# Accumulator banks for a, joined output blocks, low parts one block later: a reordering of a two-layer float32 kernel

## The chip, the cores and the metric

The kernel runs on one core of a Trainium2 chip. A core has five engines that run side by side: TensorE (PE in the profile) multiplies matrices and writes to PSUM, a memory of eight banks; VectorE (DVE), ScalarE (ACT) and GpSimd (POOL) work on elements; SyncE (SP) issues most DMAs. [...] The metric is the device time of one execution in microseconds (us).

## What is computed

Four sequences of 512 tokens of width 512 go through a slot attention of 16 heads and then through a gated feed-forward layer, each behind a layernorm and with the input added:

```python
def attn(x, Wq, Wk, Wv, Wg, Ws, Wo, gw):       # x normalised, per sequence
    q, k, v = x @ Wq, x @ Wk, x @ Wv           # heads of 64, 64, 128
    s = clip(x @ Ws, -32, 32)                  # 64 slots a head
    z = cumlogsumexp(s, over=tokens)
    g = exp(shift(z) - z); p = exp(s - z)
    hk[t] = hk[t-1] * g[t] + k[t] p[t]^T       # 64 x 64 state
    ok[t] = (q[t] * 64**-0.5) @ hk[t]
    pv = softmax(ok)
    hv[t] = hv[t-1] * g[t] + p[t] v[t]^T       # 64 x 128 state
    o[t] = pv[t] @ hv[t]
    o = o * rsqrt(mean(o*o) + 1e-5) * gw
    o = o * silu(x @ Wg)
    return o @ Wo

def ffn(x):                                    # weights rounded to fp8
    h = silu(x @ q8(gate) * gs) * (x @ q8(up) * us)
    return h @ q8(down) * ds

x = x + attn(layernorm(x), ...)
x = x + ffn(layernorm(x), ...)
```

## The kernel before, in words

**Units.** Attention is done in units (g, b): a pair of heads g (0 to 7) for a sequence b. The order is (0,0), (0,1), (1,0), (1,1), ... (7,1), and then the same for sequences 2 and 3: 32 units. first_unit() (L854) builds (0,0), attention() (L919) the other 31. The values of two pairs of heads are projected together, so units with even g also make values (L644), four blocks of 128 tokens, and last longer. The feed-forward layer follows for all four sequences.

**Precision.** A float32 matrix is split into a high and a low part (fp32r) and a third mixture of both. A projection is eight 128x512 matmuls (high and low, main()) into one bank and four (mixed()) into another; ScalarE copies the first with a factor and VectorE subtracts the second. So each projection takes two of the three "proj" banks, in turn. The weights are split on the chip the first time: load_matrix() (L233) puts a "_" item (the high part of the first piece, on ScalarE) and then pieces (two VectorE instructions and the next high part) into a queue in the program, `work`. The parts of a normalised block are made in layernorm()'s parts() (L357): low = source minus high, mixture, and then ScalarE scales the low part in place.

**Inside a unit.** slots, keys, queries project s, k and q. turn_e and turn_k transpose them (e, kn). key_states (L672) makes three running sums of k p^T, sk. query_key (L677) makes the products within a block, a, two banks of four 128x128 blocks, which VectorE masks with a triangle. slot_scores takes sk, a and e to ok; softmax (okn) and softmax_exp give weights, slot_weights turns them back (w, wT). weight_slot (L736) is to the weights what query_key is to the keys: b, two banks, masked by VectorE. read_out (L739) sums the output ov of the unit: twelve small matmuls with the states (L748), sixteen with b (L757). The output of a unit is finished inside the next: scale_output and scale_other scale ov's banks into og, turn_output (oT) transposes them and multiplies with the gate, high_output, split_output and low_output make the three parts, and project_output(n) (L825) multiplies block n with w_o: four ps_o and two ps_o_m. add_output(n) (L846) subtracts and sends the block to DRAM by an adding DMA.

**Order.** The whole program is scheduled by hand: each engine executes its instructions in the order in which Python calls issue them, and waits where a semaphore asks. Between the stages, other() (L167) takes items from `work` (pace[0] of them, 1 or 2), piece() (L172) takes items until one whose name doesn't end with "_", and need(key) (L180) all that are left of a kind. steps holds the transposes of a norm for the next sequences; next_step() does one. turned() says that the first item belongs to a normalised block (its name begins with xs_).

**Banks.** bank() (L110) gives the next of three PSUM banks in turn: for all transposes, key and value states, a and b. A transposed block of a norm keeps its bank until its parts are made; `held` makes parts() run before that bank is given out again. ps2 is a pool of two accumulator banks, "acc", in turn: ok takes one, ov two; in the feed-forward layer the sums of its output.

Of the kernel before, what the change touches and what calls it, by code (L numbers as in the profile page):

```python
# [49 lines left out]
def kernel(  # L50
# [116 lines left out]
    def other(count=None):  # L167
        for _ in range(count or pace[0]):
            if work:
                work.pop(0)[1]()  # L170
# [131 lines left out]
    def load_tokens(b, source, pool=one, tag="tokens"):  # L302

        x1[b] = pool.tile([P, NT, D], F32, tag=tag, name=f"x1_{b}")
        nc.sync.dma_start(x1[b], source[b].rearrange("(n p) d -> p n d", p=P))

    xs = {}
    whole = []

    def layernorm(b, which, n_bank=None, between=None):  # L310
# [46 lines left out]
        def parts(n):  # L357
            cols = slice(n * P, (n + 1) * P)
            hi, lo = dst[0][:, :, cols].bitcast(F32), dst[1][:, :, cols]
            src = pts[n]  # L360
            if start:
                src = whole[0][:, :, cols]
                nc.scalar.mul(dst[0][:, :, cols], src, UNDER)
            nc.vector.tensor_tensor(lo, src, hi, ALU.subtract)
            if which == 1:
                nc.vector.scalar_tensor_tensor(
                    dst[2][:, :, cols], lo.bitcast(F32), -1.0 / DELTA, hi, ALU.mult, ALU.add
                )
                nc.scalar.mul(lo, lo.bitcast(F32), 1.0 / DELTA)

        if start:
            for n in range(NT):
                measure(n)
                if n > 0:
                    normalise(n - 1)
                    transposes(n - 1)
                if n == 2:
                    between()
            normalise(NT - 1)
            transposes(NT - 1)  # L380
            return [(f"xs_{b}", lambda n=n: parts(n)) for n in range(NT)]
        key = f"xn{which}_{b}_"
# [197 lines left out]
    def diagonal_blocks(lT, rT, name):  # L580

        pa = [bank(f"ps_{name}_{h}").rearrange("p (n t) -> p n t", n=NT) for h in range(HG)]
        for n in range(NT):
# [270 lines left out]
    def first_unit():  # L854
# [15 lines left out]
        transposing = layernorm(1, 1)  # L870
        work.extend(parts)
        load_matrix("g", 0, True)
        X.values(1)
        other(3)
# [21 lines left out]
        next_step()  # L896
        other(2)
        X.gate_main(0)
# [20 lines left out]
    def attention(g, b, before, load, gated):  # L919
# [3 lines left out]
        X = Heads(g, b)  # L923
        even = g % 2 == 0

        def output(n):
# [17 lines left out]
        def running_sum():  # L944
            before.scale_other()
            X.running_sum()
            other()

# [8 lines left out]
        if even:  # L957
# [4 lines left out]
            need("v")  # L962
            X.values(0)
            before.turn_output(0)
            X.key_states()
            X.inverse()
            X.values(1)
            other()
            before.high_output(0)
            before.split_output(0)  # L970
            before.low_output(0)
            before.turn_output(1)
            X.query_key()
            X.values(2)
            before.high_output(1)
            before.split_output(1)
            before.low_output(1)
            other()
            next_step()
            X.values(3)  # L980
            other()
            next_step()
        else:
            before.turn_output(0)
            X.turn_k()
            before.turn_output(1)
            X.key_states()
            before.high_output(0)
            before.high_output(1)
            X.query_key()  # L990
            before.split_output(0)
            before.split_output(1)
            X.inverse()
            other()
        need("g")
# [22 lines left out]
        if not turned():  # L1018
            other()
        need("o")  # L1020
# [8 lines left out]
        output(2)  # L1029
        X.weight_slot()  # L1030
        other()
        output(3)
        load("o")
        other()
        next_step()
# [238 lines left out]
```

## Time and profile before

The median of three runs is 1484.76 us (1483.31 to 1485.37). The profiled execution took 1484.02 us, of which the span between its first and last instruction is 1482.3 us.

| | us |
|---|---|
| profiled run, its span | 1484.02, 1482.3 |
| first unit, (0,0), to the first ps_s of (0,1) | 63.9 |
| an even unit, ov to ov (most) | 41.8 |
| an odd unit, ov to ov (most) | 31.1 to 31.2 |
| (7,0), (7,1), (0,2), (7,2): units with transposes of a norm | 32.75, 34.7, 45.2, 33.85 |
| feed-forward, from 1201.7 | 280.6 |

How to read the lines below. A line of the timeline has the start in us, the length in us, the engine, the line of the code, the operation, output<-inputs, the shapes, and how many such instructions are merged; in brackets, how long the engine was idle before and what released it. The end of a TensorE instruction is modelled, and matmuls overlap, so what a group costs is the distance from its start to the start of the next. VectorE takes 0.6 us (a line shows 0.68) for most 128x512 instructions that stand in a row, ScalarE about 0.6.

TensorE's longest waits inside attention() are: okn for okT, 3.9 us in 12 places (1.4 at most); sk for kn, 3.2 us in 15 places (0.2 each); oT for e, 1.2; kn for xs, 1.0; xn for xs, 0.9 in 2; w for xs, 0.7.

### The profile page before, as it was taken

What the parts mean: (1) busy time and instruction counts of PE and PEld (TensorE: products, weight loads), DVE (VectorE), ACT (ScalarE), POOL (GpSimd) and SP (SyncE); (2) the same over time, 40 slices, a digit from 0 to 9 for tenths busy, and PEclk for the clock granted to TensorE, in tenths of its full rate; (3) what the DMA queues carried; (4) which work ended last, traced back from release to release, by engine and by line L of the source; (5) the groups of instructions that cost most, each with busy time, mean ns of one, the idle gap of its engine ahead of it and who ended that gap; (6) DMA issues with size and microseconds to landing.
All of it is one profiled execution on the core that took longest, in us unless ns stands there. A gap on an engine that the chain in (4) does not pass through costs nothing.

```text
span 1482.3 us, 23015 instructions
## 1 busy us (share of the span) xinstructions
PE 1449.6 (98%) x9053; PEld 1172.7 (79%) x9053; DVE 1106.9 (75%) x1968; ACT 709.3 (48%) x1214; POOL 192.5 (13%) x204
## 2 busy tenths in 40 slices
PE   8899999999999999999999999999999999999998
PEld 3588888888888887878888888888888788888886
DVE  6778868887888688877888888888888864445333
ACT  4556555655655555554544455455445543222221
POOL 2011111111111111211111111111112111000000
PEclk9999999999999999999999999999999999999999
DMA  8266556565656464446555764566555552101000
GB/s 326 81 178 212 142 139 161 198 191 150 168 175 194 120 227 121 136 117 217 142 145 139 230 164 122 154 216 171 143 178 164 142 171 29 57 1 57 1 29 29
DMA packets 80715, 212.52 MB, mean 143 GB/s; under 512 B 6152, under 2 KB 34848, under 8 KB 75424
## 3 DMA queue, kind: packets, MB, share of 16 engines
q1 hardware_dynamic: 62080, 177.49, 32.8%
q0 software_dynamic: 18528, 33.58, 15.2%
q8 instruction: 71, 1.16, 0.3%
q14 instruction: 36, 0.29, 0.1%
HBM read 107.23 MB, written 108.00 MB: 145 GB/s over the span
## 4 chain that ended last, share of the span: by engine, by line
PE 85%; DVE 11%; ACT 2%; issue 1%; DMA 0%; SPq 0%; DVEq 0%; ACTq 0%
PE ps_o L833 8%; PE ps_v L560 8%; PE ps_fg L1045 6%; PE ps_fu L1045 6%; PE ps_g L501 4%; PE ps_ov L757 4%; PE ps_s L501 4%; PE ps_o_m L833 4%; PE ps_k L501 4%; PE ps_q L501 4%; PE ps_v_m L560 4%; PE ps_fd L1089 3%; PE ps_fe L1089 2%; PE ps_b L587 2%; PE ps_a L587 2%; PE ps_g_m L524 2%
## 5 line engine op out<-in xcount | busy, mean ns | idle before, releaser
L849 POOL DMA_DIRECT2D stream<-y x128 | 110.7, 867 | 835.6 <-DVE y L848 833.5
L833 PE MATMUL ps_o<-w_o,oT 128*128 128x512 f32 x512 | 147.6, 410 | 0.0
L843 ACT ACTIVATE y<-ps_o 128x512 f32<-128x512 f32 x128 | 76.6, 598 | 113.4 <-PE ps_o L833 111.6
L501 PE MATMUL ps_g<-xs,w_g 128*128 128x512 f32 x496 | 124.9, 394 | 0.0
L560 PE MATMUL ps_v<-w_v,xs 128*128 128x512 f32 x480 | 124.5, 401 | 0.0
L1066 DVE SCALAR_TENSOR_TENSOR h<-ps_fu,scol,act 128x512 f32<-128x512 f32 x48 | 36.0, 751 | 106.5 <-PE ps_fu L1045 105.2
L501 PEld LDWEIGHTS ps_g<-xs,w_g 128*128 128x128 f32 x496 | 91.7, 188 | 20.4
L833 PEld LDWEIGHTS ps_o<-w_o,oT 128*128 128x128 f32 x512 | 89.1, 188 | 17.9
L560 PEld LDWEIGHTS ps_v<-w_v,xs 128*128 128x128 f32 x480 | 86.6, 188 | 19.1
L1045 PE MATMUL ps_fg<-xs,wf 128*128 128x512 f32 x384 | 96.5, 393 | 0.0
L1045 PE MATMUL ps_fu<-xs,wf 128*128 128x512 f32 x384 | 95.0, 389 | 0.0
L848 DVE TENSOR_TENSOR y<-y,ps_o_m 128x512 f32<-128x512 f32 x128 | 87.3, 682 | 6.7 <-ACT y L843 5.6
L1045 PEld LDWEIGHTS ps_fu<-xs,wf 128*128 128x128 f32 x384 | 72.1, 188 | 15.2
L1045 PEld LDWEIGHTS ps_fg<-xs,wf 128*128 128x128 f32 x384 | 71.1, 188 | 14.5
L823 ACT ACTIVATE oT<-oT 128x512 fp32r<-128x512 f32 x64 | 40.3, 630 | 83.9 <-DVE oT L817 83.9
L833 PE MATMUL ps_o_m<-w_o,oT 128*128 128x512 f32 x256 | 79.7, 393 | 0.1
L506 ACT ACTIVATE sg<-ps_g 128x512 f32<-128x512 f32 x62 | 37.1, 599 | 87.3 <-PE ps_g L501 87.3
L1072 ACT CAST both<-h 128x512 fp32r<-128x512 f32 x48 | 29.8, 620 | 96.4 <-DVE h L1066 96.4
L569 DVE TENSOR_TENSOR v<-v,ps_v_m 128x512 f32<-128x512 f32 x60 | 41.1, 686 | 41.7 <-PE ps_v_m L560 31.9
L772 POOL TENSOR_TENSOR rs<-rs,mhalf 128x8 f32<-128x8 f32 x32 | 58.6, 1830 | 103.7 <-DVE rs L769 100.2
L1063 ACT ACTIVATE act<-ps_fg,scol 128x512 f32<-128x512 f32 x48 | 33.0, 688 | 81.3 <-PE ps_fg L1045 81.3
L767 ACT ACTIVATE og<-ps_ov 128x512 f32<-128x512 f32 x64 | 38.1, 598 | 60.1 <-PE ps_ov L757 60.1
(166 smaller groups left out, 3271.2 us busy)
## 6 DMA issues: line engine op xcount, KB each, us to landing
stream<-y POOLq DMA_DIRECT2D x128, 256.0 KB, 6.1
split_v<-w_v SPq DMA_DIRECT2D x4, 3072.0 KB, 11.9
split_g<-w_g SPq DMA_DIRECT2D x8, 1536.0 KB, 7.4
split_o<-w_o SPq DMA_DIRECT2D x8, 1536.0 KB, 6.2
w_v<-split_v SPq DMA_DIRECT2D x4, 3072.0 KB, 15.4
w_g<-split_g SPq DMA_DIRECT2D x8, 1536.0 KB, 6.7
w_o<-split_o SPq DMA_DIRECT2D x8, 1536.0 KB, 9.8
rounded<-qw SPq DMA_DIRECT2D x36, 256.0 KB, 3.5
```

Source lines behind the costliest of these rows:

```text
L501: nc.tensor.matmul(self.p, products(self.nm, c, self.col0, i), xs[self.b][i][:, c, :], start=(i == 0 and c == 0), stop=(i == 1 and c == KC ...
L560: nc.tensor.matmul(dst, xs[b][i][:, c, n * P : (n + 1) * P], wt["v"][:, i, c * 2 * HV : (c + 1) * 2 * HV], start=(i == which[0] and c == 0 ...
L569: nc.vector.tensor_tensor(to, to, m, ALU.subtract)
L587: nc.tensor.matmul(pa[h][:, n, :], lT[rows, cols], rT[rows, cols], start=True, stop=True)
L757: nc.tensor.matmul(po[h][:, n, :], self.bb[h][:, n, :], both_v[self.b][:, n, self.v0 + h * DV : self.v0 + (h + 1) * DV], start=False, stop ...
L772: nc.gpsimd.tensor_tensor(rs, rs, mhalf.rearrange("p (h n) -> p h n", h=HG), ALU.pow)
L833: nc.tensor.matmul(dst, self.oT[:, i, h, n * P : (n + 1) * P], wt["o"][:, i, h * D : (h + 1) * D], start=(i == which[0] and h == 0), stop= ...
L843: nc.scalar.mul(y, p, 1.0 + DELTA)
L848: nc.vector.tensor_tensor(y, y, m, ALU.subtract)
L849: nc.gpsimd.dma_start(stream[self.b][n * P : (n + 1) * P, :], y, accum_op=ALU.add)
L1045: nc.tensor.matmul(pp, w[:, c * P : (c + 1) * P], xs[b][k][:, c, :], start=(c == 0 and k == 0), stop=(c == KC - 1 and k == 1),)
L1089: nc.tensor.matmul(sums[n], parts[k][:, n * P : (n + 1) * P], fw[c][2], start=(c == 0 and k == 0), stop=(c == NFC - 1 and k == 1),)
```

## The change

- diagonal_blocks() takes banks of the accumulator pool where its name begins with a (query_key), and banks from the turn for b, as before.
- attention() calls output(3) right after output(2); weight_slot and the calls of other() that stood around it come behind. load("o") is also ahead of weight_slot then.
- In even units values 0 and 1 are made one behind the other; both turn_output and query_key follow them, and the splits come behind values 2 and 3. In odd units key_states comes after query_key.
- parts() leaves the scaling of a low part to scale_low(), which runs at the start of the next block's parts; for the last block of a norm it is put at the head of `work`. The parts of the first norm: the high parts of all four blocks are made at once by first_parts(), ahead of the splits of w_g in the queue but behind values(1).
- Where `small` stands, odd units of sequences 0 and 1 (with pace 1) call piece() instead of other(). An odd unit's call behind inverse takes only items of w_o, and in odd units of sequences 0 and 1 without steps the last call is dropped. In first_unit() one call takes three items instead of two.

```diff
@@ -304,6 +304,13 @@
         x1[b] = pool.tile([P, NT, D], F32, tag=tag, name=f"x1_{b}")
         nc.sync.dma_start(x1[b], source[b].rearrange("(n p) d -> p n d", p=P))
 
+    unscaled = []
+
+    def scale_low():
+        while unscaled:
+            lo = unscaled.pop(0)
+            nc.scalar.mul(lo, lo.bitcast(F32), 1.0 / DELTA)
+
     xs = {}
     whole = []
 
@@ -357,16 +364,22 @@
         def parts(n):
             cols = slice(n * P, (n + 1) * P)
             hi, lo = dst[0][:, :, cols].bitcast(F32), dst[1][:, :, cols]
-            src = pts[n]
-            if start:
-                src = whole[0][:, :, cols]
-                nc.scalar.mul(dst[0][:, :, cols], src, UNDER)
+            src = whole[0][:, :, cols] if start else pts[n]
+            scale_low()
             nc.vector.tensor_tensor(lo, src, hi, ALU.subtract)
             if which == 1:
                 nc.vector.scalar_tensor_tensor(
                     dst[2][:, :, cols], lo.bitcast(F32), -1.0 / DELTA, hi, ALU.mult, ALU.add
                 )
-                nc.scalar.mul(lo, lo.bitcast(F32), 1.0 / DELTA)
+                unscaled.append(lo)
+                if n + 1 == NT:
+                    work.insert(0, (f"xs_{b}", scale_low))
+
+        def first_parts():
+            for n in range(NT):
+                cols = slice(n * P, (n + 1) * P)
+                nc.scalar.mul(dst[0][:, :, cols], whole[0][:, :, cols], UNDER)
+            return [(f"xs_{b}", lambda n=n: parts(n)) for n in range(NT)]
 
         if start:
             for n in range(NT):
@@ -378,7 +391,7 @@
                     between()
             normalise(NT - 1)
             transposes(NT - 1)
-            return [(f"xs_{b}", lambda n=n: parts(n)) for n in range(NT)]
+            return first_parts
         key = f"xn{which}_{b}_"
         todo = [(key + "m", lambda n=n: measure(n)) for n in range(NT)]
         todo.insert(2, (key + "0", lambda: normalise(0)))
@@ -579,7 +592,11 @@
 
     def diagonal_blocks(lT, rT, name):
 
-        pa = [bank(f"ps_{name}_{h}").rearrange("p (n t) -> p n t", n=NT) for h in range(HG)]
+        if name[0] == "a":
+            pa = [ps2.tile([P, T], F32, tag="acc", name=f"ps_{name}_{h}") for h in range(HG)]
+        else:
+            pa = [bank(f"ps_{name}_{h}") for h in range(HG)]
+        pa = [p.rearrange("p (n t) -> p n t", n=NT) for p in pa]
         for n in range(NT):
             cols = slice(n * P, (n + 1) * P)
             for h in range(HG):
@@ -868,9 +885,9 @@
         for _ in range(7):
             piece()
         transposing = layernorm(1, 1)
-        work.extend(parts)
+        X.values(1)
+        work.extend(parts())
         load_matrix("g", 0, True)
-        X.values(1)
         other(3)
         X.slots()
         other(1)
@@ -894,7 +911,7 @@
         other(2)
         X.query_key()
         next_step()
-        other(2)
+        other(3)
         X.gate_main(0)
         piece()
         X.slot_scores()
@@ -922,6 +939,7 @@
 
         X = Heads(g, b)
         even = g % 2 == 0
+        small = other if even or b > 1 or pace[0] > 1 else piece
 
         def output(n):
             before.project_output(n)
@@ -944,7 +962,7 @@
         def running_sum():
             before.scale_other()
             X.running_sum()
-            other()
+            small()
 
         X.keys(running_sum)
         load("k")
@@ -961,37 +979,38 @@
                 other(1)
             need("v")
             X.values(0)
+            X.values(1)
             before.turn_output(0)
+            before.high_output(0)
+            before.turn_output(1)
+            before.high_output(1)
             X.key_states()
             X.inverse()
-            X.values(1)
+            X.query_key()
             other()
-            before.high_output(0)
+            X.values(2)
             before.split_output(0)
             before.low_output(0)
-            before.turn_output(1)
-            X.query_key()
-            X.values(2)
-            before.high_output(1)
-            before.split_output(1)
-            before.low_output(1)
             other()
             next_step()
             X.values(3)
+            before.split_output(1)
+            before.low_output(1)
             other()
             next_step()
         else:
             before.turn_output(0)
             X.turn_k()
             before.turn_output(1)
-            X.key_states()
             before.high_output(0)
             before.high_output(1)
             X.query_key()
+            X.key_states()
             before.split_output(0)
             before.split_output(1)
             X.inverse()
-            other()
+            if work and work[0][0] == "o":
+                other()
         need("g")
         X.gate_main(0)
         if not even:
@@ -1016,7 +1035,7 @@
         X.value_states()
         X.softmax()
         if not turned():
-            other()
+            small()
         need("o")
         before.project_output(0)
         X.softmax_exp()
@@ -1027,11 +1046,12 @@
         X.softmax_sum()
         next_step()
         output(2)
-        X.weight_slot()
-        other()
         output(3)
         load("o")
-        other()
+        X.weight_slot()
+        small()
+        if even or b > 1 or steps:
+            other()
         next_step()
         X.read_out()
         return X
```

## The prediction

> **What bounds the kernel now.** I read the shares of busy time and the chain of waits first, then busy time by stage, then TensorE's own waits, and last the timeline of TensorE inside single units.
>
> ```profile
> PE 1449.6 (98%) x9053; PEld 1172.7 (79%) x9053; DVE 1106.9 (75%) x1968; ACT 709.3 (48%) x1214; POOL 192.5 (13%) x204
> ...
> PE 85%; DVE 11%; ACT 2%; issue 1%; DMA 0%; SPq 0%; DVEq 0%; ACTq 0%
> ```
>
> By stage (after the stretch and its length: busy us and instructions of PE, weight loads, VectorE, ScalarE, GpSimd; clock; DMA share; GB/s):
>
> ```profile
> 0.00:63.90 63.90, 50.74 (x233) 28.19 (x233) 43.59 (x86) 29.66 (x49) 9.24 (x20) 0.97 0.55 202
> 63.90:543.30 479.40, 476.05 (x3198) 389.57 (x3197) 383.79 (x659) 268.00 (x468) 70.31 (x65) 1.00 0.58 174
> 543.30:655.90 112.60, 108.20 (x742) 87.56 (x742) 93.14 (x174) 62.13 (x109) 20.75 (x24) 1.00 0.42 112
> ```
>
> TensorE is the bound nearly everywhere: of the 32.7 us that it idles (1482.3 - 1449.6), 13.2 lie in the first unit (63.90 - 50.74) and 4.4 between 543 and 656 us, where the next pair's tokens are normalised; in the first run of ordinary units it is 3.35 in 479. By idle time there is little to win. But a busy TensorE need not be at its pace, so I read start to start. The end of unit (2,1), a unit with even g:
>
> ```profile
> 244.60 1.17 PE L833 MATMUL ps_o<-w_o,oT 128*128 128x512 f32 x4
> 245.61 0.63 PE L833 MATMUL ps_o_m<-w_o,oT 128*128 128x512 f32 x2
> 246.17 1.16 PE L587 MATMUL ps_b<-wT,eT 64*128 64x128 f32 x16
> 247.26 1.20 PE L833 MATMUL ps_o<-w_o,oT 128*128 128x512 f32 x4
> 248.30 0.62 PE L833 MATMUL ps_o_m<-w_o,oT 128*128 128x512 f32 x2
> 248.85 0.94 PE L748 MATMUL ps_ov<-sv,wT 64*128 64x128 f32 x12
> 249.72 2.05 PE L757 MATMUL ps_ov<-v,b 128*128 128x128 f32 x16
> ```
>
> Four ps_o in an unbroken stream take 0.91 us (242.88 to 243.79) and two ps_o_m 0.46. Here they take 1.04 (247.26 to 248.30), since a small matmul came before, and 0.55 (245.61 to 246.17 and 248.30 to 248.85), since one follows. Every excursion from the wide matmuls to the small ones costs about 0.22 us that counts as busy. The middle of the odd unit (3,0):
>
> ```profile
> 261.11 0.62 PE L577 MATMUL ps_oT<-ident,og 128*128 128x128 f32 x4
> 261.95 0.57 PE L601 MATMUL ps_sk<-e,kn 128*64 128x64 f32 x12 [0.22 <-ACT kn L670]
> 262.45 1.28 PE L587 MATMUL ps_a<-qT,kT 64*128 64x128 f32 x16
> 263.66 2.11 PE L501 MATMUL ps_g<-xs,w_g 128*128 128x512 f32 x8
> ```
>
> oT takes 0.84 where its neighbours take 0.44: sk waits for ScalarE's copy of kn, at a true price of 0.40. And a takes 1.21 instead of the 1.09 of even units: its second bank is the one from which VectorE still reads oT. The first unit:
>
> ```profile
> 40.04 1.13 PE L587 MATMUL ps_a<-qT,kT 64*128 64x128 f32 x14 [0.83 <-DVE sk L614]
> 44.48 1.12 PE L347 MATMUL ps_xn<-ident,xn 128*128 128x128 f32 x4 [3.31 <-DVE xs L364]
> 45.38 4.84 PE L514 MATMUL ps_g<-xn_whole,raw_g 128*128 128x512 f32 x8
> ...
> 59.82 1.16 PE L587 MATMUL ps_b<-wT,eT 64*128 64x128 f32 x16 [0.89 <-DVE wT L734]
> 60.81 0.39 PE L748 MATMUL ps_ov<-sv,wT 64*128 64x128 f32 x4
> ```
>
> a waits for the bank that VectorE is still reading sk from, then xn for the bank of the block before it, whose parts stand late in VectorE's queue; and g takes 4.78 us to the next start instead of 3.43 (54.90 to 58.33).
>
> **What the Trainium skill says.** "Perfetto Trace Analysis", Summary: the profiler window per engine type, says that a TensorE end is an estimate; so I take only starts. "TensorE: Matmul & The Clock Gate", Part 1, says that the clock falls to half after an idle window of some 3.4 us: that fits g's 1.35 us extra behind the wait of 3.31. Its Part 1 also says that ScalarE and VectorE are strict FIFO; the trace agrees: at 33.52 ScalarE waits 1.48 us for VectorE with the low part of a block, and the next block's high part, ready long before, starts after it. "TensorEngine Tiling (Array Packing)", Key Properties, says that changing the tiling mode drains TensorE; the excursions above show 0.22 us, though which part is the tiling and which the data type, no run here shows.
>
> **Part by part.** All sums are against the profiled execution: span 1482.3, run 1484.02; the median 1484.76 lies 0.74 above it. 31 units are built by attention(): 15 with even g, 16 with odd.
>
> *Blocks 2 and 3 together.* Today from the ps_o_m before b to the last ps_ov group: 249.72 - 245.61 = 4.11 us. After: 0.46 + 0.91 + 0.56 to the start of b, then b and ov. The last ov needs b after VectorE's mask; the first unit has this order, and there it starts 1.94 after b (61.76 - 59.82): three quarters of it PE work, the rest the wait for VectorE. Sum 3.87, saving 0.24. VectorE must be free then: y of block 2 ends 2.96 after the start of its ps_o (247.56 - 244.60); y of block 3, after ScalarE, ends near 4.05; b's mask can start at 2.94 + 1.19 = 4.13. It fits by 0.1. The pieces of other work that stood between now follow b. Bounds: 0.42 if the mask cost nothing, 0.09 if it starts 0.15 late. 29 units: -7.0. In (7,0) and (7,2) a block's transposes stand between b and ov, and wait for the parts that VectorE gets only after b's mask: 3.15 us after b, today hidden under block 3 but for 0.55. With block 3 gone from there each loses about 1.3 (bounds 0 and 1.6): +2.6.
>
> *Even units.* Values 0 and 1 run unbroken; oT 0, oT 1, sk, a become one excursion: 1.958 falls to 1.813 and one entry of 0.09 goes, 0.25 with the small remainder. 15 x 0.25 = -3.8. The splits move behind values 2 and 3, far ahead of the output blocks that need them.
>
> *Odd units.* a, now in accumulator banks that the previous unit's output released during keys, runs ahead of sk: kn's copy (ends 261.90) hides under a's 1.09, and no bank is shared with oT: 0.40 + 0.12 = 0.52. qT is ready at 261.11, a could start at 261.55. Bounds 0.40 and 0.62. VectorE does a's mask before sk's sums and ends both near 264.8, as today. 15 units (without (7,1)): -7.8. The other() behind inverse goes too, so VectorE reaches okT earlier: the gap of 0.08 before okn in nine odd units ends, with 0.2 in (7,0): -0.9. In (7,2) two pieces held okT 1.26 us; they now stand behind softmax, where they delay the release of block 0's bank by some 0.5: -0.8.
>
> *Low parts a block later.* (7,1): from the e transposes at 585.29 to g at 591.78 the small work takes 6.49 us. At 577.0 ScalarE gets a low part that must wait for VectorE until 579.40; behind it stands eT's copy, so VectorE starts on eT at 580.55 instead of about 579.75, and everything up to the parts of the last block (586.59) is 0.8 late. A second low part, from 588.04, holds the copy of e, for whose bank oT waits. With the low part a block later neither waits: kn's stall falls from 1.17 to 0.33, oT's from 1.43 to 0.3, a starts behind qT near 587.8, g near 589.4: -2.4. (0,2): there two such waits delay the silu and y of block 0; w's wait of 0.96 and the block before it (0.27) shrink by 0.9.
>
> *First unit.* The high parts of all four blocks (4 x 0.55) fill ScalarE's idle 20.2 to 23.1 us, so VectorE works from 29.3 on, where it idled 2.8, 1.2 and 1.7 us. I followed its queue with the durations shown: a block's two parts 1.33, two by 31.9, the third by 33.3; sk when TensorE has it (34.8) and its inverse by 36.9; the fourth block by 38.3; the next batch's first block, after ScalarE's high part, 40.1 to 41.4; a masked by 43.1; the second block by 44.4; a piece of w_g by 47.5; okT 48.15, sv 49.0. On TensorE a follows xn at once (its banks are new), xn follows a at 39.8, g runs 40.2 to 43.65 at full clock. okn waits for sv as it does now: 49.15 instead of 54.43, -5.3. Bounds 3.5 (two of the stalls only) and 6.5 (w_g's piece not ahead of okT).
>
> *Whole pieces.* I counted the queue through two groups: an odd unit makes four calls instead of six, but each takes its "_" item along, and after (1,1) the queue holds what it holds today (q_ q g_ g g), so no weight is asked for before it is split. In the second half five items instead of six leave the queue per odd unit; the rest of up to 5 is gone by (7,3). load("o") ahead of b brings its DMA on SP's queue, or its pieces, a microsecond earlier; nothing waits there. In (0,1), though, one piece of w_g is left over from the first unit, both o pieces then fall between keys' products, 1.35 us more of VectorE before kT; kn, today 0.1 us free (72.50 to 72.65), waits: +1.2 (bounds 0 and 1.4).
>
> **Sum:** -5.3 - 7.0 + 2.6 - 3.8 - 7.8 - 0.9 - 0.8 - 2.4 - 0.9 + 1.2 = -25.1. 1484.76 - 25.1 = 1459.7.
>
> **Rivals.** (1) Only the stalls go: what I call an excursion's price belongs to each small group, so joining brings nothing and b's mask is exposed. Then blocks 2 and 3 and the even units give 0 instead of -10.8: -14.3, 1470.5. Against it: equal groups differ by their neighbours (1.958 and 1.813 for values). (2) VectorE is further ahead than I count, and (7,0), (7,2) and (0,1) lose nothing: 2 x 1.54 + 1.2 = 4.3 more, 1455.4. For it: each unit that is shorter on TensorE also frees VectorE of pieces; against it: xn there needs a part that is queued behind b's mask. (3) Slower: in all 31 units b's mask stands behind block 3's y on VectorE, which stands behind ScalarE, with TensorE waiting at the last ov. 25 us are eaten where it comes 0.8 us later than I place it; at 1.2 us, 31 x 1.2 = 37 against 25, 1497. For it: my slack is 0.1 us. Against: block 3's y has nothing ahead of it on ScalarE, and the moved pieces stand behind. (4) The new order only moves the stalls to later ones, no change: 1484.
>
> **Chances.** Forecast 0.66; rival 1 0.16; rival 2 0.10; rival 3 0.06; rival 4 0.02. About 0.2% (3 us) can be told from no change. Faster 0.92, same 0.02, slower 0.06. The forecast alone spans 1454 to 1466 by its bounds; the range reaches over rivals 1 and 2: 1452 to 1472.
>
> **What would show it.** Right: b directly before ov, the last ov group 1.9 to 2.0 us after b; values 0 and 1 at 2.72 each start to start; no wait of sk for kn; odd units near 30.3 us and even near 41.3 instead of 31.1 and 41.8 from ov to ov; the first s of (0,1) near 58.6 instead of 63.9; xn after b in (7,0) waiting 2 us. Wrong: the last ov 2.5 us or more after b; s, k or q waiting for weights; a waiting for its accumulator bank.

## The result and the profile after

The changed kernel takes 1490.92 us in the median of six runs (1488.13 to 1492.39), the kernel before 1484.47 beside it (1483.31 to 1486.09): 1.0041 times as long, with a 95% interval from 1.0029 to 1.0054. The forecast was 1459.7 us, a gain of 25; the kernel became 6.5 us slower instead. The profiled execution has a span of 1489.5 us, 7.2 more than before. The page of the changed kernel (shares of busy time; then the chain of waits), and its busy time by stage, in the columns of the stage lines of before:

```profile
PE 1448.1 (97%) x9053; PEld 1168.6 (78%) x9053; DVE 1106.0 (74%) x1968; ACT 714.0 (48%) x1214; POOL 193.9 (13%) x204
...
PE 77%; DVE 15%; ACT 4%; issue 3%; DMA 0%; SPq 0%; DVEq 0%
```

```profile
0.00:59.16 59.16, 48.99 (x233) 27.19 (x233) 42.43 (x84) 30.11 (x50) 9.64 (x20) 1.00 0.59 218
59.16:543.00 483.84, 474.93 (x3193) 386.62 (x3193) 383.11 (x658) 269.54 (x467) 70.76 (x65) 1.00 0.57 172
```

TensorE is busy for 1.5 us less and the span is 7.2 longer: TensorE idles 8.7 us more. The first unit is 4.7 us shorter (63.90 before). In the stretch of ordinary units behind it, TensorE idles 8.9 us (483.84 - 474.93) instead of 3.35. The chain that ended last has given 8% of the span from TensorE to VectorE, ScalarE and issue.

TensorE's waits in the changed kernel (what waited, for what, us in total, times, longest):

```profile
PE ps_o L850 <- ACT y L860: 4.3, 19, 0.2
PE ps_xn L354 <- DVE xs L369: 4.1, 2, 2.1
PE ps_kn L590 <- DVE kT L541: 2.6, 3, 1.7
...
PE ps_o L850 <- DVE w_o L262: 1.5, 1, 1.5
PE ps_g_m L537 <- ACT sg L519: 1.3, 6, 0.4
PE ps_oT L590 <- ACT e L682: 1.0, 3, 0.4
```

The two long waits of before that the prediction named are gone from this list: okn for okT (3.9 us in 12 places) and sk for kn (3.2 in 15). In their place stand waits of which the prediction has only one, xn for xs. To see what each costs, I divided every unit at five starts of TensorE: the first ps_s, ps_e, the first ps_g, the first ps_ok, the ps_o of block 2, and the next unit's ps_s. The differences, after minus before, in us:

| Step of the prediction | forecast | found |
|---|---|---|
| first unit | -5.3 | -4.75 |
| blocks 2 and 3, 29 units | -7.0 | +4.8 |
| xn between b and ov, (7,0) and (7,2) | +2.6 | +6.9 |
| even units, e to g, without (0,1) | -3.5 | -1.6 |
| odd units, e to g, without (7,1) | -7.8 | -4.5 |
| even units, g to ok, without (0,1) | 0 | +5.7 |
| okn's gaps; (7,2) okT | -0.9; -0.8 | -0.7; -1.3 |
| (7,1) | -2.4 | -2.5 from e to g, +2.0 at block 0 |
| (0,2), ok to block 2 | -0.9 | -0.9 |
| (0,1) | +1.2 | +1.7 at kn, +1.9 from g to ok |

"Found" adds to +6.8; the stretches not named and the feed-forward layer make the rest of the 7.2. Three rows are large and of the wrong sign or size: the joined blocks, the xn behind b, and the gates of even units.

**The joined blocks.** The end of unit (3,0) in the changed kernel, TensorE and, of VectorE, only the mask of b (L608):

```profile
275.15 1.20 PE L850 MATMUL ps_o<-w_o,oT 128*128 128x512 f32 x4
276.19 0.62 PE L850 MATMUL ps_o_m<-w_o,oT 128*128 128x512 f32 x2
277.03 1.19 PE L850 MATMUL ps_o<-w_o,oT 128*128 128x512 f32 x4 [0.23 <-ACT y L860]
278.06 0.62 PE L850 MATMUL ps_o_m<-w_o,oT 128*128 128x512 f32 x2
278.61 1.16 PE L604 MATMUL ps_b<-wT,eT 64*128 64x128 f32 x16
279.61 0.84 PE L765 MATMUL ps_ov<-sv,wT 64*128 64x128 f32 x12
279.81 1.29 DVE L608 TENSOR_TENSOR b<-ps_b,tri 128x512 f32<-128x512 f32 x2 [0.23 <-PE ps_b L604]
280.55 2.05 PE L774 MATMUL ps_ov<-v,b 128*128 128x128 f32 x16
```

From b to the last ov it is 1.94 us (280.55 - 278.61), the forecast to the digit, so VectorE's mask is in time. What fails stands above b: from its start to the next start, the ps_o_m of block 2 should cost 0.46 and costs 0.84, and the ps_o of block 3 costs 1.03 instead of 0.91, as behind a small matmul. The two blocks need four banks and the "proj" pool has three. The wait and the slower group behind it give back what the join saves: from block 2 to the next unit, 12 of the 29 units come out as long as before (within 0.04 us) and 17 are 0.26 to 0.30 longer.

**The gates of even units.** (2,0) in the changed kernel, TensorE, VectorE and ScalarE together:

```profile
190.42 0.63 ACT L840 ACTIVATE oT<-oT 128x512 fp32r<-128x512 f32 x1 [3.43 <-DVE oT L834]
...
192.62 1.99 PE L514 MATMUL ps_g<-xs,w_g 128*128 128x512 f32 x8
192.89 0.69 DVE L834 SCALAR_TENSOR_TENSOR oT<-oT 128x512 fp32r<-128x512 f32 x1
193.62 0.63 ACT L840 ACTIVATE oT<-oT 128x512 fp32r<-128x512 f32 x1 [2.08 <-DVE oT L834]
194.15 1.15 ACT L519 ACTIVATE sg<-ps_g 128x512 f32<-128x512 f32 x2
...
194.78 1.20 PE L537 MATMUL ps_g_m<-xs,w_g 128*128 128x512 f32 x4 [0.18 <-ACT sg L519]
```

ScalarE takes its instructions in order. The second low part (L840) is ahead of the copy of the first gate product (L519), and waits for VectorE's split (L834), which stands behind the last values' subtraction now. So the copy, possible near 191.9 when the first ps_g was done, comes at 194.15, and the second ps_g_m waits for that bank.

**xn behind b.** (7,0) in the changed kernel, TensorE; then busy time and clock in two stretches of it (the clock stands ahead of the last two columns):

```profile
571.01 1.16 PE L604 MATMUL ps_b<-wT,eT 64*128 64x128 f32 x16
574.24 0.83 PE L354 MATMUL ps_xn<-ident,xn 128*128 128x128 f32 x4 [2.06 <-DVE xs L369]
575.00 1.65 PE L765 MATMUL ps_ov<-sv,wT 64*128 64x128 f32 x12
576.58 2.68 PE L774 MATMUL ps_ov<-v,b 128*128 128x128 f32 x16
```

```profile
570.00:574.20 4.20, 2.17 (x21) 1.52 (x19) 3.86 (x9) 1.63 (x3) 2.42 (x4) 1.00 1.00 127
574.20:577.70 3.50, 3.46 (x21) 2.94 (x22) 2.37 (x4) 0.60 (x1) 0.00 (x0) 0.55 0.88 134
```

The wait is the predicted one (xn starts 3.23 us after b; 3.15 were forecast). But the clock falls to half right behind it (it is 0.55 in the mean of the second stretch), and the first ov group takes 1.58 us to the next start, where it takes 0.94 in (3,0) above.

### The profile page after: what moved, and what is told of

It is laid out like the page before. It is cut to its first block, busy times and chain, and to the rows that moved or that the text cites. A ratio compares the mean times of both kernels' runs of the same rounds, so it can differ in the third digit from the quotient of the medians.

```text
span 1489.5 us, 22990 instructions
## 1 busy us (share of the span) xinstructions
PE 1448.1 (97%) x9053; PEld 1168.6 (78%) x9053; DVE 1106.0 (74%) x1968; ACT 714.0 (48%) x1214; POOL 193.9 (13%) x204
## 4 chain that ended last, share of the span: by engine, by line
PE 77%; DVE 15%; ACT 4%; issue 3%; DMA 0%; SPq 0%; DVEq 0%
PE ps_o L850 9%; PE ps_fg L1065 6%; PE ps_g L514 6%; PE ps_fu L1065 5%; PE ps_v L573 5%; PE ps_ov L774 4%; PE ps_g_m L537 3%; PE ps_o_m L850 3%; PE ps_s L514 3%; PE ps_k L514 3%; PE ps_q L514 3%; PE ps_fd L1109 3%; PE ps_b L604 2%; PE ps_v_m L573 2%; PE ps_fe L1109 2%
## 5 line engine op out<-in xcount | busy, mean ns | idle before, releaser
L840 ACT ACTIVATE oT<-oT 128x512 fp32r<-128x512 f32 x64 | 40.5, 633 | 92.9 <-DVE oT L834 91.9
L581 ACT ACTIVATE v<-ps_v 128x512 f32<-128x512 f32 x60 | 35.7, 595 | 73.3 <-PE ps_v L573 73.3
```

## The experiments

Eleven kernels, each timed in three rounds beside the kernel before, whose median was 1484.61, 1485.00 and 1485.14 us in the three sets.

| kernel | us | ratio to before, 95% interval |
|---|---|---|
| changed, blocks 2 and 3 apart again | 1476.71 | 0.9944 (0.993 to 0.9959) |
| changed, splits and low parts earlier | 1499.91 | 1.0091 (1.0074 to 1.0108) |
| changed, a spare bank for block 3 | 1479.76 | 0.996 (0.9945 to 0.9975) |
| changed, norm's last step behind ov | 1484.19 | 0.9994 (0.9986 to 1.0003) |
| changed, low parts behind the gate's copy | 1483.74 | 0.9987 (0.998 to 0.9994) |
| before, a ahead of sk alone | 1481.74 | 0.9976 (0.9965 to 0.9986) |
| changed, four mends with the spare bank | 1463.97 | 0.9857 (0.984 to 0.9873) |
| changed, the other mends, blocks apart | 1466.29 | 0.9871 (0.9856 to 0.9886) |
| four mends, piece ahead of block 2 | 1471.86 | 0.9911 (0.9895 to 0.9928) |
| four mends, one item in (0,1) | 1463.24 | 0.9853 (0.9838 to 0.9867) |
| before, the norm's parts alone | 1478.58 | 0.9956 (0.9941 to 0.9971) |

**Blocks apart again.**

```diff
         output(2)
+        X.weight_slot()
+        small()
         output(3)
         load("o")
-        X.weight_slot()
-        small()
         if even or b > 1 or steps:
```

> The changed kernel with b between output blocks 2 and 3 again, all else as changed. Theory (the joined blocks cost: block 3 waits for one of the three proj banks in ordinary units, and in (7,0) and (7,2) a norm's transposes wait 2.1 us and the clock halves): from the third block to the next unit's s falls by 0.25 in most odd units, by 0 to 0.25 in even ones, and by about 3.4 in (7,0) and (7,2); in all 11.7 us, so 1479 to 1480, and faster than the kernel before by 5. Rival (the joining itself is right and the loss comes from elsewhere, as my sum had it at -4.4): 1491 plus 4, 1495.

1476.71: the theory's direction, and 14.2 us less than the changed kernel. The stretch from block 2 to the next unit falls by 8.6 us in odd and 1.8 in even units, of which (7,0) and (7,2) have 5.7. That is less than the 6.8 expected of these two: in (7,0), xn still waits 1.46 us for VectorE, where it waited 0.47 before. Another 3.7 us come from elsewhere: in (1,0), (3,0), (5,0) and in (2,2), (2,3), (4,2), (6,3) the small work between e and g is 0.37 to 0.67 shorter each, since a piece of the queue stands between the blocks again. This part was not expected; the piece-ahead run below tests it. (In the profile the first unit is 2.0 us shorter too. Its length varies from 56.9 to 59.7 us between the ten kernels that share its code, so such a difference between two profiles says little, here and below.)

**Splits and low parts earlier.** In even units the second split and its low part move from behind values 3 to behind values 2.

```diff
             before.low_output(0)
+            before.split_output(1)
+            before.low_output(1)
             other()
             next_step()
             X.values(3)
-            before.split_output(1)
-            before.low_output(1)
             other()
```

> The changed kernel with both blocks' splits of an even unit behind values 2, ahead of values 3. Theory (the second split stands behind values 3 on VectorE, its low part holds ScalarE ahead of the gate's copy, and the gate's banks come late): the gates of even units fall from 0.1 to 0.6 us over the kernel before to nothing, about -5.5 without (0,1) and (0,2), so 1485 to 1486. Rival (the gates wait because of values 3 itself, whose subtraction is late now that values 0 and 1 go first): the gates stay, 1491.

1499.91: slower by 9 us than the changed kernel, as neither the theory nor the rival had it. The same place in (2,0):

```profile
191.96 0.63 ACT L840 ACTIVATE oT<-oT 128x512 fp32r<-128x512 f32 x1 [0.70 <-DVE oT L834]
192.49 0.58 ACT L581 ACTIVATE v<-ps_v 128x512 f32<-128x512 f32 x1
192.97 0.59 ACT L519 ACTIVATE sg<-ps_g 128x512 f32<-128x512 f32 x1
...
193.12 1.20 PE L537 MATMUL ps_g_m<-xs,w_g 128*128 128x512 f32 x4 [1.13 <-ACT v L581]
```

Now the low part holds the copy of values 3 (L581) and the gate waits for that bank, 1.13 us. The kind of cause was right, a low part that waits for VectorE at the head of ScalarE's queue, but the cure was backward: VectorE can't be earlier there, so the low part must be asked for later.

**A spare bank for block 3.** Its ps_o takes one of the three banks that transposes use, where no block of a norm is kept in one.

```diff
-        def project_output(self, n):
+        def project_output(self, n, spare=False):
             name = f"ps_o_{self.u}_{n}"
-            p = ps3.tile([P, D], F32, tag="proj", name=name)
+            p = bank(name) if spare else ps3.tile([P, D], F32, tag="proj", name=name)
...
         output(2)
-        output(3)
+        before.project_output(3, not steps and not held)
+        before.add_output(3)
```

> The changed kernel, but block 3's first bank is taken from the three banks in turn, which a no longer uses, in units without a norm's blocks. Bank theory: the 0.14 (even) or 0.39 (odd) between block 2 and block 3 go, and block 3's four ps_o fall from 1.03 to 0.91; b to the last ov stays 1.94; 0.25 to 0.5 us in some 26 units, -10, 1481. Rival (b's mask on VectorE is the bound, and TensorE only waits elsewhere if block 3 is sooner): what is won ahead of b is lost behind it, the last ov more than 2.2 us after b, 1489 to 1491.

1479.76, 11.2 us less than the changed kernel; 10 were expected. The end of (3,0) in this kernel:

```profile
274.93 0.62 PE L850 MATMUL ps_o_m<-w_o,oT 128*128 128x512 f32 x2
275.39 1.07 PE L850 MATMUL ps_o<-w_o,oT 128*128 128x512 f32 x4
276.29 0.61 PE L850 MATMUL ps_o_m<-w_o,oT 128*128 128x512 f32 x2
276.84 1.16 PE L604 MATMUL ps_b<-wT,eT 64*128 64x128 f32 x16
```

0.46, 0.90 and 0.55 from start to start: the forecast's three terms (0.46, 0.91, 0.56). In the 29 ordinary units the stretch is now 0.22 to 0.27 us shorter than before, as forecast (0.24). So the price of an excursion was right and the missing bank took it. In the changed kernel the first product of block 3 waits for either of two readers, as the semaphore that this instruction waits on tells: in 12 units VectorE's, and it starts 0.05 us after VectorE has read block 1's ps_o_m; in 19 ScalarE's, and it starts 0.05 after ScalarE's y of block 2, with VectorE done 0.19 to 0.48 ahead of that start. If the three banks went strictly in turn, it would be the bank of block 1's ps_o_m in every unit; in these 19 they don't. From the ps_o_m ahead to this product it is some 0.85 us there, 0.55 to 0.61 in the twelve. The 19 are (7,0), (7,2) and the 17 units that came out longer. The spare bank ends both kinds of wait.

**The norm's last step behind ov.**

```diff
-        next_step()
         X.read_out()
+        next_step()
         return X
```

> The changed kernel with the last transposes of a norm in a unit behind the sums of its output instead of between b and them; only (7,0) and (7,2) have any there. Theory (3.45 us lost in each by a wait of 2.1 and the half clock after it): the wait is covered by the output's sums, no half clock, -3.4 in each, 1484. Rival (VectorE and ScalarE are late there anyway, the wait moves to (7,1)'s first transposes): -1 to -2 in all, 1489.

1484.19: 6.7 less. (7,0) and (7,2) lose 3.83 and 3.82 us, (7,1) gives 1.0 back, where kn now waits for the later part of the block. Without the wait there is no half clock in either unit. The length of the wait alone doesn't decide whether the clock falls (the last section says what does): the spare-bank kernel has the same wait of 2.06 us in (7,0),

```profile
569.91 0.63 PE L354 MATMUL ps_xn<-ident,xn 128*128 128x128 f32 x4 [2.06 <-DVE xs L369]
570.47 0.94 PE L765 MATMUL ps_ov<-sv,wT 64*128 64x128 f32 x12
```

and its ov runs at full clock, 0.87 to the next start.

**Low parts behind the gate's copy.** In even units both low parts go where odd units have them.

```diff
             X.values(2)
             before.split_output(0)
-            before.low_output(0)
...
             X.values(3)
             before.split_output(1)
-            before.low_output(1)
...
         X.gate_main(0)
-        if not even:
-            before.low_output(0)
-            before.low_output(1)
+        before.low_output(0)
+        before.low_output(1)
```

> The changed kernel, with both low parts of the previous output in even units issued behind the copy of the first gate product, where odd units have them. Theory (in even units the low parts wait in ScalarE's queue for VectorE's splits and hold the gate's copy, so the second gate product waits for its bank): the gates' stretch of the even units, now 7.6 us longer than before in sum, loses about 5.5 of it and the time is near 1485.5; TensorE no longer waits for ScalarE's gate copy there. Rival (VectorE is late for other reasons and the low parts only show it): the wait moves to the second gate's copy or to the silu, the time stays at 1490 to 1491.

1483.74, 7.2 less than the changed kernel; the even units' stretch from g to ok gives 6.8 of it (forecast 5.5), of which (0,1) 1.9. (2,0) in this kernel:

```profile
188.98 0.60 ACT L519 ACTIVATE sg<-ps_g 128x512 f32<-128x512 f32 x1 [2.17 <-PE ps_g L514]
189.48 1.14 ACT L840 ACTIVATE oT<-oT 128x512 fp32r<-128x512 f32 x2
189.64 1.98 PE L514 MATMUL ps_g<-xs,w_g 128*128 128x512 f32 x8
```

The copy runs as soon as the product is there, the low parts behind it find their splits done, and the wait of ps_g_m for sg is gone from the list of waits. VectorE was not late in itself; the rival falls.

**a ahead of sk alone**, on the kernel before: the accumulator banks for a, and in odd units

```diff
             before.turn_output(1)
-            X.key_states()
             before.high_output(0)
             before.high_output(1)
             X.query_key()
+            X.key_states()
```

> The kernel before, with one part of the change alone: a in accumulator banks, and in odd units ahead of sk. Theory: each odd unit loses the wait of sk for kn and the shared bank, 0.41 us as measured between e and g in the changed kernel, and (1,0), (3,0), (5,0) gain too, since pieces of weights still stand where they stood before: 15 x 0.41 = 6.2 less, 1478.4. Rival 1 (the late high part in these three units comes from the new order itself): 12 x 0.41 = 4.9 less, 1479.7. Rival 2 (the accumulator banks come free too late, ok or ov waits): no gain, 1484.

1481.74, half the expected gain. From e to g all 15 odd units lose 0.39 to 0.41 us, (1,0), (3,0) and (5,0) too: so it isn't the new order that makes e late in these three. But 11 of the 15 give 0.22 to 0.30 back at okn, whose wait for okT grows from 3.9 to 6.7 us in 12 places: TensorE is earlier, and VectorE isn't, with a piece of the queue behind the inverse. In the changed kernel, which takes only w_o's pieces there, the wait is gone. The two parts need each other. (7,1) becomes 1.1 longer, and that is the clock: in this profile it is at half from 586.73 to 590.15 us, and a takes 1.65, sk 0.84 and the first g 2.58 us there instead of 1.09, 0.50 and 1.95 in (3,1) of the same kernel. The first unit is 1.85 shorter in this one profile.

**Four mends together**: the spare bank, the norm's last step behind ov, the low parts behind the gate's copy, and

```diff
             X.inverse()
+            if work and work[0][1] is scale_low:
+                other(1)
             if work and work[0][0] == "o":
                 other()
```

which lets (7,1) pass the norm's item at the head of the queue and reach w_o's piece; in the changed kernel block 0 of this unit waits for it:

```profile
603.41 0.50 PE L850 MATMUL ps_o<-w_o,oT 128*128 128x512 f32 x1 [1.47 <-DVE w_o L262]
```

> The changed kernel with four mends: block 3's first product in a bank of the other pool, the last step of a norm behind the readout, the low parts behind the first gate's copy, and in odd units the scaling of a norm's last low part taken from the head of the queue ahead of the pieces of w_o. Theory (the faults are independent but for (7,0) and (7,2), which the first two share): -11.2 - 6.7 + 3.1 - 5.5 - 1.5 = -21.8, near 1469. Rival (one late engine stands behind all of them, VectorE with the pieces; mending one wait brings out the next): 1474 or more.

1463.97, 27 us less than the changed kernel and 21 less than the kernel before; 1469 were expected, and the rival's 1474 falls: the faults don't hide each other. (7,1) loses 1.7 at block 0. Part of the surplus over the expectation may be the first unit, 1.75 us shorter here in the profile.

**The same with blocks apart**

> As the run before, but output blocks 2 and 3 apart again, with b between them, in place of the spare bank. Theory: 1476.7 (blocks apart alone) - 5.5 (low parts) - 2 (what the norm's step still gains in (7,0) and (7,2)) - 1.5 (w_o's piece in (7,1)) = near 1467.7, so within 2 us of the spare bank's version: joined blocks are worth what they were said to be worth only with a fourth bank, and little even then. Rival (with VectorE relieved, joined blocks bring their 0.24 us per unit): the spare bank's version is faster by 4 us or more.

1466.29: apart is 2.3 us slower than joined with the spare bank, between the theory (at most 2) and the rival (4 or more). In 29 units joined is 0.23 to 0.26 better from block 2 to the next unit, 6.9 in all; against it stand the seven units in which e or kn is late, 3.8, and (7,0) and (7,2), 0.5. Joined blocks bring what they should, and cost elsewhere because of where their pieces fall.

**The piece ahead of block 2** (on the four mends):

```diff
         next_step()
+        early = not (steps or held or turned())
+        if early:
+            small()
         output(2)
...
         X.weight_slot()
-        small()
+        if not early:
+            small()
```

> The version with four mends and the spare bank (1463.97), with one more move: in units without a norm's steps the piece of rounding or splitting that the joined blocks pushed behind b is taken ahead of block 2 again. Theory (the pieces behind b are what makes e and kn late in (1,0), (3,0), (5,0) and in (2,2), (2,3), (4,2), (6,3), since both then fall between two units): the stretch from e to g loses 0.55 in the three odd units and 0.4 to 0.7 in the four even ones, 3.8 in all, 1460.2; b's mask stays on time since VectorE is free between the subtractions of blocks 1 and 2. Rival (VectorE isn't free there): the piece pushes block 3's subtraction and b's mask back, ov waits 0.5 or more in each such unit, and the time is 1470 or more.

1471.86: the time is the rival's. But each was right about its part. From e to g the seven units get back 0.36 to 0.71 each, 3.8 in all, as expected: pieces behind b are the cause of the late e and kn. But the stretch behind block 2 grows by 12.2 us. Its largest wait, and the end of (3,1):

```profile
PE ps_ov L774 <- DVE b L608: 14.6, 24, 0.8
```

```profile
304.94 1.16 PE L604 MATMUL ps_b<-wT,eT 64*128 64x128 f32 x16
...
306.88 1.28 DVE L608 TENSOR_TENSOR b<-ps_b,tri 128x512 f32<-128x512 f32 x2
...
307.62 1.16 PE L774 MATMUL ps_ov<-v,b 128*128 128x128 f32 x8 [0.84 <-DVE b L608]
```

A piece of two VectorE instructions ahead of the blocks puts the mask 1.94 us behind the start of b instead of 1.20 (279.81 - 278.61 in (3,0) of the changed kernel), and ov waits 0.84. So a mask that comes 0.74 later costs this unit 0.74: this is the wait of the prediction's third rival, at the price that it named, and the changed kernel doesn't pay it, since its pieces stand behind.

**One item in (0,1)** (on the four mends): one item of the queue instead of two between the products of keys.

> The version with four mends and the spare bank (1463.97), with one item instead of two from the queue between the two products of keys in (0,1). Theory (the two pieces of w_o on VectorE ahead of the subtraction of kT are the 1.7 us that kn waits there): one piece goes, kn's wait falls by 1.2 to 1.4, 1462.6; the piece is made later in the same unit, where nothing waits. Rival (what is late is the piece wherever it stands, since w_o is needed in this unit): the wait moves to block 0, no gain.

The profile has (0,1) shorter by 1.35 us (2.0 less at kn, 0.65 more at the gates), so the two pieces of w_o were the cause of kn's wait; the first unit was 0.95 longer in the same profile, and the times, 1463.24 with 1462.64 to 1464.02, can't be told from 1463.97: a gain in the whole is not shown.

**The norm's parts alone**, on the kernel before: scale_low(), first_parts() and the first unit's order, without the rest.

> The kernel before, with another part of the change alone: a norm's low part scaled a block later, and the first norm's high parts made at once with the first unit's calls that go with it; a stays in the turn's banks, the units' orders stay. Theory: the first unit gains what the accumulator banks alone (1.85 there) have left of 4.75, some 2.9 to 3.4; (7,1) gains 2.0 to 2.5 between e and g, and loses no time at block 0 since the call behind the inverse still takes any item; (0,2) gains 0.9 ahead of block 2: 1484.8 - 6 to 6.8 = about 1478.4. Rival (the gain in (7,1) and (0,2) belongs to the new order of the units and not to the low parts): the first unit's gain alone, 1481.7.

1478.58, where 1478.4 was expected, though not by the same sum (the profiled span, 1477.7, is 4.6 below that of before). The first unit is 4.35 us shorter; (7,1) loses 1.62, (0,2) 0.87, (0,1) pays 2.2, of which 2.0 at kn. So the rival falls: the changed kernel has these gains, and kn's wait in (0,1), from this part and not from the new orders. Whether this part and a's banks add up in the first unit is not shown: 4.35 and 1.85 alone make 6.2, the changed kernel has 4.75, and the kernels that share its code lie from 4.2 to 7.0.

## Why the prediction was wrong

The direction was wrong, with most of the prices right. Of the some 32 us between the sum forecast (-25.1) and the one found (+6.8), a missing bank is 11.8, low parts ahead of a copy 6.8, the xn behind b 4.3, and pieces that came behind b 3.8; smaller misses make the rest. What failed, in the prediction's own steps:

- *Blocks 2 and 3 together*, "Sum 3.87, saving 0.24": the failing step. It looked at VectorE's mask, whose slack of 0.1 us held, and took the ps_o_m and ps_o in front of b at the pace of an unbroken stream without asking for their banks. Four products in three banks: +4.8 instead of -7.0 in 29 units. With a fourth bank the stretch is 0.22 to 0.27 shorter.
- *Even units*, "The splits move behind values 2 and 3, far ahead of the output blocks that need them": true of the output blocks, but the low parts that follow the splits stand ahead of the gate's copy in ScalarE's queue. Costed at nothing, worth 6.8 us by the run that moved them, 1.9 of it in (0,1). The rest of that row is (0,2), where 0.9 stays: a wait of xn for VectorE. I named no one behind the waiting instruction, which the prediction's own reading of the first-in-first-out queue at 33.52 us should have made me do.
- *(7,0) and (7,2)*, "each loses about 1.3": the wait came as worked out; the loss is 3.45 each. 1.55 of the excess is the clock, which fell to half behind a wait of 2.06: so much shorter is the stretch in the spare-bank kernel, which has the same waits there at full clock. The other 0.6 is the missing bank and a wait slightly longer than I had it.
- *Odd units*, 0.52 each: measured 0.41, near the lower bound. The 0.12 of a came (1.09 instead of 1.21). What was mis-sized is the 0.40: it took the oT ahead at its neighbours' 0.44, but with a behind it this oT takes 0.55, so 0.29 goes. In (1,0), (3,0) and (5,0) nothing was left, since ScalarE does the high part of a piece ahead of e. (3,0) in the changed kernel:

```profile
259.33 0.62 ACT L255 ACTIVATE w_v<-raw_v 128x512 fp32r<-128x512 f32 x1
...
259.85 0.58 ACT L519 ACTIVATE qT<-ps_q 128x512 f32<-128x512 f32 x1
...
260.33 0.57 ACT L682 COPY e<-ps_e 128x512 f32<-128x512 f32 x1
...
260.95 0.66 PE L590 MATMUL ps_oT<-ident,og 128*128 128x128 f32 x4 [0.34 <-ACT e L682]
...
261.54 1.16 PE L604 MATMUL ps_a<-qT,kT 64*128 64x128 f32 x16
...
262.63 0.57 PE L618 MATMUL ps_sk<-e,kn 128*64 128x64 f32 x12
```

  a to sk is 1.09 as forecast and sk no longer waits; the second oT waits 0.34 for a bank in front of it instead.
- *Whole pieces*: "The pieces of other work that stood between now follow b" was put at nothing. It costs 3.8 us in the seven units, by the run that moved them.
- *(7,1)*: -2.5 against -2.4 where I looked, though the norm's parts alone give only 1.7 of it, so the agreement is in part luck; and +2.0 where I didn't: the call that takes only pieces of w_o sees the norm's item at the head and does nothing, so block 0 waits.

Right were the first unit (-4.75 against -5.3, with -4.2 to -7.0 in the kernels that share its code), the pace of b to ov, the values' 0.25 in even units (0.23 to 0.29 in those not otherwise late), okn's gaps, the 0.9 of (0,2) ahead of block 2, and the direction of (0,1). With four faults mended the kernel takes 1463.97, 21 us less than before, where the forecast was 25 less. Three of the four are waits in a queue or for a bank that the prediction passed over; the fourth, xn behind b, it had, but too small. Rival 4, stalls only moved, is nearest in its mechanism; it had been given a chance of 0.02.

## What to carry to other kernels

When matmul groups are joined, count the banks that they need between them before counting the switches that they save: here a join is worth 0.24 us and a missing bank costs 0.25 to 0.5. For each instruction that a move makes wait, name the next three in its engine's queue and who waits for those; where the producer can't be earlier, ask later, as the low parts behind the gate's copy did. And a piece of background work that moves from one gap to the next doesn't cost nothing: it meets whatever else is there.

## What the hardware showed that was not expected

TensorE's clock fell to half behind a wait of 2.06 us, in (7,0) and in (7,2) of the changed kernel, though 1.72 us in its first unit (okn for sv, at 49.69) left it whole. The Trainium skill, "TensorE: Matmul & The Clock Gate", Part 1, puts the fall behind an idle window of some 3.4 us and says that the window runs freely, so that the same kernel varies from run to run.

The traces agree with the second. In the changed kernel each of the two falls inside the program lasts 3.413 us, and the stretches at full clock ahead of them are 559.79 and 593.92 us, which is 164.0 and 174.0 times that: the changes of the clock stand on a fixed grid. Busy time on this grid, in the changed kernel around the wait of (7,0), then in the spare-bank kernel around the same wait, which lies across the border at 568.58:

```profile
571.11:574.52 3.41, 1.35 (x19) 1.18 (x20) 3.14 (x6) 1.17 (x3) 2.04 (x3) 1.00 1.02 131
574.52:577.94 3.42, 3.42 (x22) 2.86 (x20) 2.05 (x4) 0.60 (x1) 0.00 (x0) 0.50 0.84 128
```

```profile
565.17:568.58 3.41, 2.68 (x22) 1.95 (x22) 3.10 (x9) 1.64 (x3) 2.40 (x4) 1.00 1.03 132
568.58:571.99 3.41, 2.08 (x21) 1.82 (x22) 3.34 (x6) 0.60 (x1) 0.56 (x1) 1.00 1.02 142
```

The first window idles 2.06 us (3.41 - 1.35), and the next is at half clock. In the spare-bank kernel the wait is shared out, the two windows idle 0.73 and 1.33, and the clock stays; the 1.72 us in the first unit lie across a border too. With the grid laid from the first change of the clock in each of the thirteen traces, TensorE idles 1.74 us or more, by the modelled ends, in 24 of 5568 windows, nine of them inside the program and the others at its end. The clock is at half in the window behind each of the 24 and behind no other, and the most idle of the others has 1.73. So these traces don't bear out the 3.4 us as a bound for one gap: a window that was idle for about half of its length was enough, and whether a wait of 2 us costs the clock depends on where it falls on the grid. The grid doesn't start with the program: the first change of the clock comes at 10.9 to 15.6 us in the thirteen traces. The times fit: the three other executions of the spare-bank kernel had a mean clock of 0.997 instead of 0.999 and took 2.5 to 2.9 us longer than the profiled one, near what two falls cost (1.55 each).
